# Steps of sorting and of sums queued behind the last instruction of three engines, and ternary weights made among the sorted groups, in a four-layer decoder

## The chip, the cores and the metric

One core of a Trainium2 chip runs the whole decoder as one kernel. The metric is the time of one execution on the device in microseconds (us). The kernel before has a median of 3301.1 us in 15 runs, from 3294.51 to 3314.32. About 0.2% (6.6 us) is what a measurement of this kernel can tell from no change.

## What is computed

A decoder of four layers, each with self-attention, cross-attention and a feed-forward part, and a layer normalization after each of the twelve residual sums. `x` and the context have 128 sequences of 64 tokens of 128 numbers: 8192 tokens, all in float32. The parts that this change touches:

```python
# layer 0, "attention" is a mixture of experts: 8 experts, the best 2 of each token
x = _layernorm(x + _L0_attn_ref(x, gate_w, gate_b, w1, b1, w2, b2))
# layer 0, cross-attention with one head over 64 keys
x = _layernorm(x + _L0_xattn_ref(x, ctx_1024, Wq, bq, Wk, bk, Wv, bv))
# layer 0, feed-forward 128 -> 512 -> 128 with ternary weights
def _ternary(w):
    scale = jnp.maximum(jnp.mean(jnp.abs(w)), 1e-08)
    w_t = jnp.clip(jnp.round(w / scale), -1.0, 1.0)
    return w + jax.lax.stop_gradient(w_t - w)
x = _layernorm(x + _L0_ffn_ref(x, W1, b1, W2, b2))
...
# layer 3: masked cross-attention with 16 heads, then a switch layer (best 1 of 8 experts, with a capacity)
x = _layernorm(x + _L3_xattn_ref(x, ctx_1024, ctx_1024, mask, ...))
x = _layernorm(x + _L3_ffn_ref(x, wg, W1, b1, W2, b2))
```

## The kernel before, in words

**Engines and names.** PE (TensorE) multiplies; `V`, `A` and `G` are VectorE (DVE in the profile), ScalarE (ACT) and GpSimd (POOL); SP issues most DMAs. `x` stays in on-chip memory as 16 chunks `X[0]` to `X[15]` of 512 tokens, each four tiles of 128 tokens.

**Who sets the order.** A scheduler of the tile framework chooses the order of the instructions of each engine from what the Python code traces; it may move an instruction ahead of others traced earlier. Each engine then runs its list strictly in that order. Inside `with tc.issue_after(ins):` every instruction that is traced comes behind `ins` in the list of `ins`'s engine; this is an order, not a wait on a result. `Sorted.after` (used as `moe.after(...)`) is the same for the last instruction that the sorting code kept in `s.pe`, `s.dve`, `s.sp`, `s.gather` or `s.act_ins`.

**The stages** (list `steps` at the end of `tile_decoder`): `moe_top2`, `xattn_single` (cross-attention and ternary feed-forward of layer 0 in one loop), `attn_diff`, `xattn_causal`, `ffn_routed`, `attn_alibi`, `xattn_padded`, `ffn_conv`, `attn_scan`, `xattn_masked`, `ffn_switch`. Ahead of each, `load_weights(n)` (L286) loads a later layer's weights from SP into one of three buffers of the pool `wts`.

**The mixture of experts** (class `Sorted`, `moe`, `moe_top2`) sorts the chosen tokens of a batch of chunks (chunks 0 to 4, then 5 to 15) into groups of 256 rows of one expert: 27 and 51 groups. `all_groups` (L872) walks over the 78 groups: `load` brings the expert's weights (`rw`, 512 KB, SP), `rows` gathers the 256 rows (`aux`, indirect DMAs of POOL, L757, from an index copy `rat` of DVE, L755), `turn` transposes them (`ebT`, L768 and L770), `hidden` and `output` multiply (L782, L795), and `yo` goes to `l_rout` in DRAM (L797). After each group come the `between` hook (here `context`, L917 on: it loads the context) and steps of two generators: the plan of the next batch and the finish of the last one.

**The finish** (`finish`, L803 to L870) is one generator step per tile of 128 tokens plus some at the end. A step copies the row numbers of the tile (`fat`, L815, DVE; four buffers), gathers the two experts' rows (`got`, L817, POOL, two buffers each), adds them to `x` for an earlier tile (L827, L829, DVE), and for each full chunk makes the statistics (L839, L840), the Newton steps of a reciprocal square root (`rsqrt_steps`, L348), and the normalization: `ln_apply` (L371) writes `X[c]` with four instructions, on ACT (`on_act`, L378, with one more DVE product `lns`, L375), or on DVE or POOL (L380). The finish calls it with `on_act=True`. `moe.stretch = 2` leaves about half of batch 0's finish over; `moe_sums` (the generator `moe_end`) holds that remainder and all of batch 1's finish: 11 chunks. `moe_done(c)` (L936) runs it until chunk `c` is normalized.

**The single-head stage** (`xattn_single`, L985 to L1116) runs iterations i from -3 to 17. One iteration traces, for several chunks at once: scores of i+1, the transposed `x` (`turned`) of i-2, the weights, projections of i+2 (bank `v_ps`, L1003), `hidden` of i-2 (first ternary product, L1093, GELU on ACT), `values` of i (L1048; residual `r` L1054; normalization on ACT), `sources` of i+3 (calls `moe_done(i+3)`, transposes the context and `x`, L325 and L332), `output` of i-2 (second ternary product `y`, L1103; residual L399; normalization on DVE for chunks below 8, on POOL from 8 on), with four calls of `summed` between them, one step of `moe_end` each. The ternary weights are made by `ternary(n)` (L1062 to L1080) in iterations -3 and -2; two bias vectors are spread over three bfloat16 rows by `bias_rows` (L966).

**The masked stage** is `mha` (L1130 on) with `aside=kept`: between its parts it runs the first sorting steps of the switch layer (`switch.plan(0)`), each queued behind `seen`, the last instruction of one part of the attention, and `spread`, the last one of a projection.

Of the kernel before, what the change touches and what calls it, by code (L numbers as in the profile page):

```python
# [12 lines left out]
F32 = mybir.dt.float32  # L13
# [4 lines left out]
ALU = mybir.AluOpType  # L18
# [212 lines left out]

@with_exitstack
def tile_decoder(ctx: ExitStack, tc: tile.TileContext, a, out):
    nc = tc.nc
# [6 lines left out]
    dram = ctx.enter_context(tc.tile_pool(name="dram", bufs=1, space=DRAM))  # L243

    mm = nc.tensor.matmul
    V, A, G = nc.vector, nc.scalar, nc.gpsimd


    x_in = a["x"].rearrange("(c t p) d -> c p t d", t=TPC, p=P)
# [35 lines left out]

    def load_weights(n):  # L286

        if 0 < n < 11:
            name = LAYER_WEIGHTS[n - 1]
            parts = []  # L290
            for o in range(0, _NBLOCKS[name], 8):
                k = min(8, _NBLOCKS[name] - o)
                parts.append(work("wts", (P, k, P), f"w_{name}{o}"))
                nc.sync.dma_start(out=parts[-1], in_=a["w_" + name][:, o : o + k, :])
            W[n] = parts[0] if len(parts) == 1 else parts

    def table(name, shape, src):
        t = work("tab", shape, name)
# [6 lines left out]
    def row(n):  # L305
        return rows[:, _ROW_AT[n][0] : _ROW_AT[n][1]]
# [4 lines left out]
    ident = const.tile([P, P], F32, tag="ident", name="ident")  # L311
    make_identity(nc, ident)


    def bank(name):
        return psB.tile([P, 512], F32, tag="m", name=name)
# [155 lines left out]
    class Sorted:  # L472
# [3 lines left out]

        def __init__(s, which, top, batches, src, wg, bias, act, cap=None, store=False, scattered=None):
            s.which, s.top, s.batches, s.src, s.wg, s.bias, s.act, s.cap, s.store = which, top, batches, src, wg, bias, act, cap, store
            s.at, s.loaded, s.done, s.carry = {}, {}, set(), None
# [322 lines left out]
        def finish(s, b):  # L802


            where, share, _, _ = s.at[b]
            K, rows_, cs = s.top, s.count(b) * GR, s.batches[b]
            nt = TPC * len(cs)
            got, sums, ends = {}, {}, []

            def read(n):  # L810
                i, t = divmod(n, TPC)
                if t == 0:
                    got[i] = [work(tag, (P, TPC, D), "got") for tag in ("oT", "ye")[:K]]
                at = sm.tile([P, 2], I32, tag="fat", name="fat", bufs=4)[:, :K]
                s.dve = V.tensor_copy(at, where[:, :, n])  # L815
                for k in range(K):
                    s.gather = G.indirect_dma_start(  # L817
                        out=got[i][k][:, t, :], out_offset=None, in_=s.rout[b][:, :],
                        in_offset=bass.IndirectOffsetOnAxis(ap=at[:, k : k + 1], axis=0), bounds_check=rows_ - 1, oob_is_err=False,
                    )  # L820

            def add(n):
                i, t = divmod(n, TPC)
                if t == 0:
                    sums[i] = work("r", (P, TPC, D)), sm.tile([P, TPC, 6], F32, tag="fst", name="fst")
                r, st = sums[i]
                V.scalar_tensor_tensor(r[:, t, :], got[i][0][:, t, :], share[:, 0, n : n + 1], X[cs[i]][:, t, :], ALU.mult, ALU.add)  # L827
                if K == 2:
                    V.scalar_tensor_tensor(r[:, t, :], got[i][1][:, t, :], share[:, 1, n : n + 1], r[:, t, :], ALU.mult, ALU.add)  # L829
                s.dve = V.bn_stats(st[:, t, :], r[:, t, :])  # L830

            def end(i):
                r, st = sums.pop(i)
                got.pop(i)
                f = sm.tile([P, 4, TPC], F32, tag="fln", name="fln")
                mv = f[:, :2].rearrange("p a t -> p (a t)").rearrange("p (t a) -> p t a", a=2)
                v, y = f[:, 2], f[:, 3]
                for t in range(TPC):
                    V.bn_aggr(mv[:, t, :], st[:, t, :])  # L839
                s.dve = V.tensor_scalar(v, mv[:, :, 1], LN_EPS, None, ALU.add)  # L840
                yield
                for ins in rsqrt_steps(v, TPC, y):
                    s.dve = ins
                    yield
                ln_apply(cs[i], r, mv, y, s.store, on_act=True)
                s.done.add(cs[i])
                yield

            for n in range(nt + LATE + 3):
                if n < nt:  # L850
                    read(n)
# [74 lines left out]
            with moe.after(moe.sp):  # L926
                moe.sp = nc.sync.dma_start(out=CIN[c // 8][:, c % 8 * TPC : (c % 8 + 1) * TPC, :], in_=c_in[c])

    moe.between = context

    def moe_top2():
        for _ in moe.plan(0):
            pass
        moe.all_groups()

    def moe_done(c):  # L936

        while c not in moe.done:
            next(moe_end)


    CTX = [None] * NC
# [38 lines left out]
        return both[:32, 0, :], both[:32, 1, None, :].to_broadcast([32, 4, D])  # L981


    def xattn_single():
        w = W[1]  # L985
        scale = 1.0 / math.sqrt(D)

        st = {}
        bv = bias_rows(row("l0xbv"), 0, "bv1")
        ring = work("e", (P, 4, TPC, D), "v1")  # L990

        def sources(c):
# [62 lines left out]
            layernorm(c, r, on_act=True)  # L1055


        b2 = bias_rows(row("l0fb2"), 1, "b2t")
        tern = W[2]
        wt = work("tab", (P, 2, FK, P), "tern")  # L1060

        def ternary(n):  # L1062
            src = tern[:, 4 * n : 4 * n + 4, :].rearrange("p k m -> p (k m)")
            t = work("tmp", (P, 512), "absw")
            s = sm.tile([P, 1], F32, tag="terns", name="terns")
            A.activation(t, src, AF.Abs)
            V.tensor_reduce(s, t, AX.X, ALU.add)
            ps = bank("tern_ps")
            mm(ps[:, 0:1], sq[:, 2, :], s, start=True, stop=True)

            V.tensor_scalar(s, ps[:, 0:1], 1.0 / (D * FF), 1e-8, ALU.mult, ALU.max)
            V.reciprocal(s, s)
            df = wt[:, n].rearrange("p k m -> p (k m)")
            V.tensor_scalar(df, src, s, None, ALU.mult)
            V.tensor_scalar(df, df, -1.0, 1.0, ALU.max, ALU.min)

            V.tensor_scalar(df, df, 12582912.0, None, ALU.add)
            V.tensor_scalar(df, df, 12582912.0, None, ALU.subtract)
            V.tensor_tensor(df, df, src, ALU.subtract)
            V.tensor_tensor(df, df, src, ALU.add)  # L1080

        def summed(_):
            next(moe_end, None)

        def turned(c):
            st[c] = {"xT": transposed(X[c], "xT")}
# [21 lines left out]
        for i in range(-3, NC + 2):  # L1108
            for step, c in (
# [2 lines left out]
            ):  # L1112
                if step == summed or 0 <= c < NC:
                    step(c)
            if i in (-3, -2):
                ternary(i + 3)  # L1116


    half = const.tile([P, 816], BF16, tag="half", name="half")
# [7 lines left out]
    def rows32(t, g):  # L1127
        return t[32 * g : 32 * g + 32]

    def mha(prepare, wv, finish, mask=None, diff=False, aside=lambda c, k, seen: None):  # L1130

# [165 lines left out]
        on, late, spread = range(NC), (), None  # L1297
        for c in range(-2, NC + 1):
            last = finish(c - 1, st[c - 1]) if c - 1 in on else iter(())
            behind = None  # L1300
            if c in on:
                behind = weights(c, 0)
# [6 lines left out]
            aside(c, 0, (behind, spread))  # L1309
# [5 lines left out]
            aside(c, 1, (seen, spread))  # L1315
            if c in on:
                weights(c, 1)
                behind = values(c, 0)
            aside(c, 2, (behind, spread))
            if c + 1 in on:  # L1320
                scores(c + 1, 1)
                split_maxima(c + 1)
            if c + 2 in on:
                spread = project(c + 2)
            next(last, None)

            seen = maxima(c + 1) if c + 1 in on else None
# [4 lines left out]
            aside(c, 3, (seen, spread))  # L1332
            st.pop(c - 1, None)
        for _ in late:
            pass
# [577 lines left out]
                k = min(16, (n - o) // P)  # L1913
                nc.sync.dma_start(out=x[o : o + k * P, :].rearrange("(k p) d -> p k d", p=P), in_=z[:, None, :].to_broadcast([P, k, D]))

    def kept(c, k, seen):

        last = SWITCH_BATCHES[0][-1]
        n = c - last - 2
        late = [(2, 2, 3, 3), (3, 3, 1, 1), (1, 1, 1, 1), (1, 2, 1, 1), (1, 2, 1, 2), (99, 0, 0, 0)]  # L1920
        steps = 0 if c < 2 else k == 2 if n < 0 else late[n][k]
        with ExitStack() as behind:
            for i in seen:
                if i:
                    behind.enter_context(tc.issue_after(i))
            for _ in range(steps):
                next(switch_begin, None)

    def ffn_switch():
# [34 lines left out]
```

## Time and profile before

| | |
|---|---|
| median of 15 runs | 3301.1 us (3294.51 to 3314.32) |
| the profiled execution | 3298.13 us, span 3296.4, granted clock of TensorE 0.950 |
| PE, DVE, ACT, POOL busy | 2906.6, 2017.0, 1642.5, 1466.0 us |
| groups of the mixture of experts | 53 to 439.5 us, PE busy 336.05 of 386.5 |
| single-head stage | 439.5 to 757 us |
| masked attention, then the switch layer | about 2720 to 3035, then to the end |

How to read it: the page cuts the span into 40 slices of 82.4 us and gives each engine's busy share in tenths; PEclk is the clock that TensorE was granted. Further down it lists groups of instructions: line, engine, operation, what is written `<-` what is read, shapes, count, then busy us and mean ns, and after the bar the engine's idle time just ahead of them and what ended it. A timeline row has start, duration, engine, line, operation, count, and in brackets the idle time ahead. In a table by stretch each row has a stretch, its length, the busy us of PE, PEld (weight loads), DVE, ACT, POOL with counts, then the granted clock, the DMA share and GB/s. A wait line has the engine, the line that waited, the releaser, then us in total, times, longest.

### The profile page before, as it was taken

To read this page: it belongs to the slowest core of one execution; us is meant where nothing else is said; L and a number is where in the kernel's file an instruction comes from. 1 tells how busy PE (TensorE), PEld (TensorE's weight loads), DVE (VectorE), ACT (ScalarE), POOL (GpSimd) and SP (SyncE) were. 2 spreads that over 40 slices of the span, in tenths; PEclk is the share of its full clock that TensorE was granted. 3 is DMA by queue.
4 is the path that set the end of the run, shared out by engine and by line. 5 is a ranking of instruction groups with operands and counts; after the bars stand their busy time and mean duration, and the time that the engine had idled before them with its cause. 6 is when DMAs were issued, how large, how long until landed. Compare 5 with 4: busy or idle time off the path is not lost. (4 is left out here: it accounts for less than half of the span.)

```text
span 3296.4 us, 110598 instructions
## 1 busy us (share of the span) xinstructions
PE 2906.6 (88%) x47136; PEld 2114.6 (64%) x47136; DVE 2017.0 (61%) x7344; ACT 1642.5 (50%) x3138; POOL 1466.0 (44%) x1500
## 2 busy tenths in 40 slices
PE   5888888998899899999999989998999569998983
PEld 3788755565666677766677767774444337766883
DVE  3732256766777566632346665666888886676245
ACT  3443355765544465433345545553445555654443
POOL 2565554334555444311134453557566323436144
PEclk9999988999999899999999999999999789998997
DMA  4567731000000200000000000000000000002684
GB/s 132 158 192 210 226 89 31 20 8 3 3 3 16 78 4 4 6 1 1 1 15 4 4 5 4 4 6 7 1 1 2 8 1 16 18 15 71 191 239 136
DMA packets 142461, 159.26 MB, mean 48 GB/s; under 512 B 16720, under 2 KB 118096, under 8 KB 141968
## 3 DMA queue, kind: packets, MB, share of 16 engines
q1 hardware_dynamic: 128064, 123.66, 13.0%
q0 software_dynamic: 13184, 27.03, 3.2%
q8 instruction: 370, 6.06, 0.8%
q10 hardware_dynamic: 720, 1.50, 0.1%
q14 instruction: 123, 1.01, 0.1%
HBM read 121.45 MB, written 30.67 MB: 46 GB/s over the span
## 5 line engine op out<-in xcount | busy, mean ns | idle before, releaser
L1213 DVE TENSOR_REDUCE m<-s_ps 128x8 f32<-128x512 f32 x640 | 397.4, 683 | 141.7 <-PE s_ps L1441 50.2
L1262 ACT ACTIVATE e<-t_ps 128x512 f32<-128x512 f32 x640 | 330.0, 601 | 149.4 <-PE t_ps L1255 149.0
L1280 PE MATMUL av_ps<-vx,e 128*64 128x18 f32 (+1 forms) x10240 | 338.6, 216 | 8.0 <-issue 7.7
L1280 PEld LDWEIGHTS av_ps<-vx,e 128*64 128x64 f32 x10240 | 320.6, 140 | 28.1 <-issue 20.9
L784 ACT ACTIVATE hT<-h_ps,aux 128x256 f32<-128x256 f32 x496 | 206.8, 470 | 248.2 <-issue 169.2
L1157 POOL TENSOR_SCALAR eb<-qT,small 128x512 f32<-128x512 f32 x80 | 131.3, 1641 | 424.5 <-ACT qT L960 202.6
L817 POOL DMA_INDIRECT got<-l_rout,fat x192 | 192.1, 1001 | 218.6 <-DVE fln L839 63.5
L1243 PE MATMUL t_ps<-eb,kT 32*64 32x128 f32 x10240 | 282.7, 286 | 4.6 <-DVE m L1213 2.3
L380 POOL TENSOR_SCALAR x<-xb,lnmv,ln_y 128x128 f32<-128x128 f32 x240 | 189.3, 801 | 173.9 <-DVE ln_y L345 167.4
L782 PE MATMUL h_ps<-ebT,rw 128*128 128x256 f32 x992 | 245.7, 392 | 17.9 <-DVE ebT L770 14.6
L795 PEld LDWEIGHTS yg<-rw,hT 128*128 128x128 f32 x1984 | 241.7, 192 | 6.7
L1243 PEld LDWEIGHTS t_ps<-eb,kT 32*64 32x64 f32 x10240 | 199.5, 132 | 71.7 <-DVE m L1213 26.1
L795 PE MATMUL yg<-rw,hT 128*128 128x128 f32 x1984 | 241.9, 275 | 0.0
L1205 PE MATMUL s_ps<-eb,qT 32*64 32x256 f32 x5120 | 216.9, 397 | 19.5 <-POOL eb L1157 8.3
L757 POOL DMA_INDIRECT aux<-in_x_dram,rat x156 | 158.8, 1018 | 127.9 <-DVE rat L755 43.4
L782 PEld LDWEIGHTS h_ps<-ebT,rw 128*128 128x128 f32 x992 | 184.6, 196 | 43.7 <-DVE ebT L770 18.8
L380 POOL TENSOR_SCALAR x<-r,lnmv,ln_y 128x128 f32<-128x128 f32 x100 | 79.9, 812 | 293.8 <-DVE ln_y L345 246.7
L1285 DVE RECIPROCAL rc<-av_ps 128x32 f32<-128x32 f32 (+1 forms) x192 | 61.7, 321 | 238.9 <-PE av_ps L1280 238.7
L796 DVE TENSOR_TENSOR yo<-yg,aux 128x256 f32<-128x256 f32 x124 | 52.4, 422 | 251.1 <-PE yg L795 247.8
L1155 ACT ACTIVATE eb<-qT,small 128x512 f32<-128x512 f32 x160 | 106.8, 715 | 128.4 <-POOL qT L1382 123.7
L1157 POOL TENSOR_SCALAR eb<-kT,small 128x512 f32<-128x512 f32 x80 | 145.1, 1814 | 21.1 <-ACT kT L962 11.0
L1205 PEld LDWEIGHTS s_ps<-eb,qT 32*64 32x64 f32 x5120 | 113.8, 133 | 59.4 <-issue 14.8
(443 smaller groups left out, 6495.6 us busy)
## 6 DMA issues: line engine op xcount, KB each, us to landing
rw<-in_l0w_dram SPq DMA_DIRECT2D x78, 512.0 KB
rw<-in_l3w_dram SPq DMA_DIRECT2D x46, 512.0 KB
l_rout<-yo SPq DMA_DIRECT2D x124, 128.0 KB
aux<-xd SPq DMA_DIRECT2D x46, 128.0 KB
aux<-in_l0b_dram SPq DMA_DIRECT2D x78, 66.0 KB
xd<-vx SPq DMA_DIRECT2D x5, 1024.0 KB
x<-in_x_dram SPq DMA_DIRECT2D x16, 256.0 KB
cin<-in_ctx_dram SPq DMA_DIRECT2D x16, 256.0 KB
```

The costliest lines, as they stand in the source:

```text
L380: (V if on_dve else G).tensor_scalar(X[c][:, t, :], r[:, t, :], mv[:, t, 0:1], y[:, t : t + 1], ALU.subtract, ALU.mult)
L757: s.gather = G.indirect_dma_start(out=eb[:, i, :], out_offset=None, in_=x[:, :], in_offset=bass.IndirectOffsetOnAxis(ap=at[:, i : i + 1], ...
L782: s.pe = mm(ps[:, j * GR : (j + 1) * GR], w1[:, (k + j) * P : (k + j + 1) * P], ebT, start=True, stop=True)
L784: s.act_ins = A.activation(hT[k + j], ps[:, j * GR : (j + 1) * GR], s.act, bias=v[:, k + j : k + j + 1])
L795: s.pe = mm(y[:, i * P : (i + 1) * P], hT[k][:, i * P : (i + 1) * P], w2[:, k, :], start=(k == 0), stop=(k == FK - 1))
L817: s.gather = G.indirect_dma_start(out=got[i][k][:, t, :], out_offset=None, in_=s.rout[b][:, :], in_offset=bass.IndirectOffsetOnAxis(ap=at[ ...
L1157: ins = (G if h == 2 else V).tensor_scalar(dst, x, mine, None, ALU.mult)
L1205: mm(ps[g][j * S : (j + 1) * S, u * 256 : (u + 1) * 256].rearrange("p (h k) -> p h k", h=4), rows32(s["q"], g)[:, b], rows32(s["eb"], g)[: ...
L1213: last = V.tensor_reduce(s["m"][:, g, 2 * hf : 2 * hf + 2, :].rearrange("p t h -> p (t h)"), ps[g].rearrange("p (n k) -> p n k", k=S), AX. ...
L1243: mm(ps[g][i * S : (i + 1) * S].rearrange("p (a u j q) -> p a u j q", u=2, a=2, j=2)[:, :, u, j, :], rows32(s["k"], g)[:, b], rows32(s["eb ...
L1262: last = A.activation(e[:, g, :], ps[g], AF.Exp, scale=scale)
L1280: mm(av[j * S : (j + 1) * S, 8 * (u - u0) + n, :], ev[:, n // 2, n % 2, u, j, :], vx[:, 2 * (2 * hf + u) + j, n, :], start=True, stop=True,)
```

## The change

- `V`, `A` and `G` become `Recorded` engines: each keeps the last instruction that was traced on it. `behind(V, A, G)` queues a block behind the last one of each.
- Each `summed` step, each step that `moe_done` runs, and each sorting step of `kept` stands in such a block. The arguments `seen`, `behind` and `spread` of `mha` fall away.
- The ternary weights and the two bias vectors are made in 12 pieces (`made_first`), one at every second of the last 24 groups of the mixture of experts; the weights they need are loaded (`load_weights(2)`) when 30 groups are left, behind the DMAs that the groups put on SP.
- When the groups are done, `moe.slack` is set, and the rest of the finish normalizes on POOL (L380) where it did on ACT (L378).

```diff
+class Recorded:
+    def __getattr__(self, name):
+        method = getattr(self.engine, name)
+        def call(*args, **kwargs):
+            ins = method(*args, **kwargs)
+            self.last = getattr(ins, "ins", None) or self.last
+            return ins
+        return call
...
-    V, A, G = nc.vector, nc.scalar, nc.gpsimd
+    V, A, G = Recorded(nc.vector), Recorded(nc.scalar), Recorded(nc.gpsimd)
...
-        if 0 < n < 11:
+        if 0 < n < 11 and n not in W:
...
+    def behind(*engines):
+        stack = ExitStack()
+        for e in engines:
+            if e.last:
+                stack.enter_context(tc.issue_after(e.last))
+        return stack
...
-                ln_apply(cs[i], r, mv, y, s.store, on_act=True)
+                ln_apply(cs[i], r, mv, y, s.store, on_act=not s.slack)
...
-    moe.between = context
...
         moe.all_groups()
+        assert next(making, None) is None
+        moe.slack = True
...
         while c not in moe.done:
-            next(moe_end)
+            with behind(V, A, G):
+                next(moe_end)
...
+    def ternary(n):
...
+        A.activation(t, src, AF.Abs)
+        yield V.tensor_reduce(s, t, AX.X, ALU.add)
+        ps = bank("tern_ps")
+        moe.pe = mm(ps[:, 0:1], sq[:, 2, :], s, start=True, stop=True)
+        yield
...
+        V.tensor_scalar(df, src, s, None, ALU.mult)
+        yield V.tensor_scalar(df, df, -1.0, 1.0, ALU.max, ALU.min)
+        V.tensor_scalar(df, df, 12582912.0, None, ALU.add)
+        yield V.tensor_scalar(df, df, 12582912.0, None, ALU.subtract)
+        V.tensor_tensor(df, df, src, ALU.subtract)
+        yield V.tensor_tensor(df, df, src, ALU.add)
+
+    def made_first():
+        FIRST["wt"] = work("tab", (P, 2, FK, P), "tern")
+        for n in range(2):
+            yield from ternary(n)
+        FIRST["bv"] = bias_rows(row("l0xbv"), 0, "bv1")
+        yield
+        FIRST["b2"] = bias_rows(row("l0fb2"), 1, "b2t")
+        yield
+
+    making = made_first()
+
+    def before_single(left):
+        context(left)
+        if left == 30:
+            with moe.after(moe.sp):
+                moe.sp = load_weights(2)
+        if left < 24 and left % 2:
+            with behind(V, A, G), moe.after(moe.pe):
+                moe.dve = next(making, None) or moe.dve
+
+    moe.between = before_single
...
+        wt, bv, b2 = FIRST["wt"], FIRST["bv"], FIRST["b2"]
         def summed(_):
-            next(moe_end, None)
+            with behind(V, A, G):
+                next(moe_end, None)
...
-            if i in (-3, -2):
-                ternary(i + 3)
...
-    def kept(c, k, seen):
+    def kept(c, k):
...
-        with ExitStack() as behind:
-            for i in seen:
-                if i:
-                    behind.enter_context(tc.issue_after(i))
-            for _ in range(steps):
+        for _ in range(steps):
+            with behind(V, A, G):
                 next(switch_begin, None)
```

More of the change, by code (lines that the diff above doesn't have):

```diff
@@ L230, in _laid_out, with __init__ @@
     return {n: np.ascontiguousarray(a) for n, a in out.items()}
+class Recorded:
+    def __init__(self, engine):
+        self.engine, self.last = engine, None
+    def __getattr__(self, name):
[5 more added lines that the diff above has]
+        return call
 @with_exitstack
@@ L293, in load_weights @@
                 parts.append(work("wts", (P, k, P), f"w_{name}{o}"))
-                nc.sync.dma_start(out=parts[-1], in_=a["w_" + name][:, o : o + k, :])
+                ins = nc.sync.dma_start(out=parts[-1], in_=a["w_" + name][:, o : o + k, :])
             W[n] = parts[0] if len(parts) == 1 else parts
+            return ins
     def table(name, shape, src):
@@ L478, in __init__ @@
             s.which, s.top, s.batches, s.src, s.wg, s.bias, s.act, s.cap, s.store = which, top, batches, src, wg, bias, act, cap, store
-            s.at, s.loaded, s.done, s.carry = {}, {}, set(), None
+            s.at, s.loaded, s.done, s.carry, s.slack = {}, {}, set(), None, False
             s.row_tiles, s.turned, s.between, s.stretch, s.rest = {}, {}, None, 1, None
@@ L981, in bias_rows @@
         return both[:32, 0, :], both[:32, 1, None, :].to_broadcast([32, 4, D])
+    FIRST = {}
+    def ternary(n):
+        src = W[2][:, 4 * n : 4 * n + 4, :].rearrange("p k m -> p (k m)")
+        t = work("tmp", (P, 512), "absw")
+        s = sm.tile([P, 1], F32, tag="terns", name="terns")
+        A.activation(t, src, AF.Abs)
[3 more added lines that the diff above has]
+        yield
+        V.tensor_scalar(s, ps[:, 0:1], 1.0 / (D * FF), 1e-8, ALU.mult, ALU.max)
+        V.reciprocal(s, s)
+        df = FIRST["wt"][:, n].rearrange("p k m -> p (k m)")
+        V.tensor_scalar(df, src, s, None, ALU.mult)
[22 more added lines that the diff above has]
+    moe.between = before_single
     def xattn_single():
@@ L988, in xattn_single @@
         st = {}
-        bv = bias_rows(row("l0xbv"), 0, "bv1")
         ring = work("e", (P, 4, TPC, D), "v1")
@@ L1055, in values @@
             layernorm(c, r, on_act=True)
[L1058 to L1080, printed above, removed]
+        wt, bv, b2 = FIRST["wt"], FIRST["bv"], FIRST["b2"]
         def summed(_):
-            next(moe_end, None)
+            with behind(V, A, G):
+                next(moe_end, None)
         def turned(c):
@@ L1128, in rows32, with mha @@
         return t[32 * g : 32 * g + 32]
-    def mha(prepare, wv, finish, mask=None, diff=False, aside=lambda c, k, seen: None):
+    def mha(prepare, wv, finish, mask=None, diff=False, aside=lambda c, k: None):
         dh = 16 if diff else 8
@@ L1296, in mha @@
         nlam = lam_neg() if diff else None
-        on, late, spread = range(NC), (), None
+        on, late = range(NC), ()
         for c in range(-2, NC + 1):
             last = finish(c - 1, st[c - 1]) if c - 1 in on else iter(())
-            behind = None
             if c in on:
-                behind = weights(c, 0)
+                weights(c, 0)
             for _ in late:
@@ L1308, in mha @@
                 values(c - 1, 1)
-            aside(c, 0, (behind, spread))
+            aside(c, 0)
             seen = scores(c + 1, 0) if c + 1 in on else None
@@ L1314, in mha @@
                 project_v(c + 1)
-            aside(c, 1, (seen, spread))
+            aside(c, 1)
             if c in on:
                 weights(c, 1)
-                behind = values(c, 0)
-            aside(c, 2, (behind, spread))
+                values(c, 0)
+            aside(c, 2)
             if c + 1 in on:
@@ L1323, in mha @@
             if c + 2 in on:
-                spread = project(c + 2)
+                project(c + 2)
             next(last, None)
@@ L1331, in mha @@
             late = last if diff else ()
-            aside(c, 3, (seen, spread))
+            aside(c, 3)
             st.pop(c - 1, None)
```

## The prediction

> **What bounds the kernel now.** I read the page's forty slices first, then the busy table by stretch, then groups, waits and timelines of the one stage that the change rearranges. The page:
>
> ```profile
> PE   5888888998899899999999989998999569998983
> ...
> POOL 2565554334555444311134453557566323436144
> PEclk9999988999999899999999999999999789998997
> ```
>
> A slice is 82.4 us. TensorE (PE) is nearly full in most slices; POOL is nowhere near it. So TensorE sets the end, and an edit counts only by what it puts on TensorE or keeps it waiting for. The stages touched are the sorting MoE (groups from 53 to 439.5 us), the single-head stage fused with the ternary FFN (439.5 to 757, slices 6 to 9) and the masked attention (about 2720 to 3035). The table by stretch (PE, PEld, DVE, ACT, POOL busy, then granted clock):
>
> ```profile
> 520.00:540.00 20.00, 17.69 (x101) 12.59 (x101) 13.93 (x88) 12.44 (x25) 8.00 (x8) 0.74 0.12 28
> ...
> 560.00:580.00 20.00, 18.12 (x111) 10.88 (x112) 14.29 (x91) 12.19 (x26) 8.00 (x8) 0.83 0.11 27
> ...
> 640.00:680.00 40.00, 40.00 (x310) 27.61 (x312) 30.70 (x186) 32.86 (x65) 6.28 (x8) 1.00 0.01 2
> ```
>
> While the MoE's left-over sums run (to about 620) an iteration of the single-head stage is not bound by TensorE's work: the first products of `hidden` (L1093) start at 503.57 and, seven iterations later, at 636.26: 19.0 us each. Behind them they start at 651.10, 665.98, 680.51: 14.8 us each, at clock 1.00 with PE busy all the time. What holds an iteration at 19 is in the groups of 455 to 640 (busy, mean ns | idle ahead of them, releaser):
>
> ```profile
> L817 POOL DMA_INDIRECT got<-l_rout,fat x88 | 87.9, 999 | 91.9 <-DVE fln L839 62.3 <-issue 20.7 <-DVE fat L815 5.3
> L1103 PE MATMUL y<-tern,vx 128*128 128x128 f32 x256 | 40.3, 318 | 0.0
> ...
> L378 ACT ACTIVATE x<-r,lns,fln 128x128 f32<-128x128 f32 x44 | 19.9, 503 | 0.1
> ...
> L815 DVE COPY fat<-pli 128x2 int32<-128x2 int32 x44 | 7.5, 173 | 39.2 <-DMA got<-l_rout,fat 39.2
> ```
>
> One chunk's finish is eight gathers on POOL (L817); DVE stalls 39.2 us in all for gathers, ahead of the next index copy (L815). POOL's timeline shows the burst, its first and last gather and the next burst:
>
> ```profile
> 545.63 1.01 POOL L817 DMA_INDIRECT got<-l_rout,fat  x1 [9.85 <-DVE fln L839]
> 546.95 1.00 POOL L817 DMA_INDIRECT got<-l_rout,fat  x1 [0.31 <-issue]
> ...
> 554.78 1.00 POOL L817 DMA_INDIRECT got<-l_rout,fat  x1 [0.30 <-issue]
> 565.60 1.01 POOL L817 DMA_INDIRECT got<-l_rout,fat  x1 [9.82 <-DVE fln L839]
> ```
>
> A gather takes 1.30 us from start to start; then POOL idles 9.8. DVE's part: a late index copy, the residual sum of the FFN's output (L399), and that chunk's normalization on DVE:
>
> ```profile
> 558.26 0.17 DVE L815 COPY fat<-pli 128x2 int32<-128x2 int32 x1 [2.20 <-DMA got<-l_rout,fat]
> ...
> 560.06 0.68 DVE L399 TENSOR_TENSOR r<-y,x 128x512 f32<-128x512 f32 x1
> ...
> 566.21 1.09 DVE L380 TENSOR_SCALAR x<-r,lnmv,ln_y 128x128 f32<-128x128 f32 x4
> ```
>
> TensorE pays for the late L399 with a wait for the bank, and a slow stretch behind it:
>
> ```profile
> 560.79 0.37 PE L1003 MATMUL v_ps<-vx 32*128 32x512 bf16 x1 [2.54 <-DVE r L399]
> 561.09 1.20 PE L1008 MATMUL v_ps<-w_l0x,ctx 128*64 128x128 f32 x16
> 562.88 6.61 PE L1093 MATMUL h_ps<-xT,tern 128*128 128x512 f32 x8 [0.58 <-ACT xT L332]
> ```
>
> **The change, part by part.** Counts of the emitted programs: 56 normalizations `x<-r,fln` leave ACT (L378) for POOL, 14 `lns` products vanish from DVE, the multiplications and DMAs stay the same in number.
>
> *1. Order in the single-head stage (decides).* Each `summed` step is now queued behind the last instruction that VectorE, ScalarE and GpSimd got when it was traced, so the order on an engine is fixed where before the scheduler chose. In the changed program an iteration holds, on POOL: x1, two gathers, x2 x3 x4, six gathers. On DVE: L399, statistics, Newton steps, the four normalizations, then index copy #4 (#1 to #4: the copies for the four tiles of a chunk; each feeds two gathers), #1 of the next chunk, the last Newton step of `fln`, #2, #3. On PE: `hidden`, `values`, scores, transpose 1 of a chunk that waits for x1, the first three products of `y`, transposes 2 to 4 (for x2 to x4), and only then the other 13 products of `y` of `output` (each two instructions in the trace). That closes a ring: the end of `y` (call it Y) releases L399; DVE's order puts copy #4 behind the normalizations that follow L399; POOL's order puts x1 to x4 behind gathers that wait for these copies; PE's order puts the next Y behind x4. One turn, from rows:
> - Y to DVE's last normalization: in before 560.06 to 567.30 is 7.24 us, with work of other steps between. Counting only what the new order leaves there I get 6.3 to 6.9; I take 6.5.
> - copy #4: 0.17, say 0.2.
> - four gathers (#4 and the next #1): 4 x 1.30 = 5.2.
> - x1 on POOL. The same operation there, in the stage's later half, is the row below: 0.80.
>
> ```profile
> L380 POOL TENSOR_SCALAR x<-r,lnmv,ln_y 128x128 f32<-128x128 f32 x32 | 25.1, 796 | 68.9 <-PE h_ps L1093 47.0 <-DVE ln_y L345 21.9
> ```
>
> - two gathers 2.6, x2 to x4 2.4.
> - transposes 0.3.
> - 26 instructions of `y`: 3.17 at 552.71 (full clock). Ahead of them PE has now waited about 4 us. After a wait of 3.97 us (at 489.67) 18 of them took 4.21, which makes 26 of them 6.1. Between 3.2 and 6.1 I take 4.3.
>
> Sum 6.5 + 0.2 + 5.2 + 0.8 + 2.6 + 2.4 + 0.3 + 4.3 = **22.3 us** (21.0 to 24.5 by the ends of the terms). In before the ends of `y` go from 498.08 to 646.93 in eight turns, 18.6 each. So 8 x 3.7 = +30 (19 to 47). Two more iterations end the sums: about 19 against 15, and 16 against 15: +5. What goes is DVE's 39.2 us of stalls at L815 and PE's waits for L399 below; late next is POOL's x4.
>
> ```profile
> PE v_ps L1003 <- DVE r L399: 8.9, 5, 2.5
> PE y L1048 <- DVE r L1054: 4.3, 4, 2.0
> ```
>
> *A rule on the clock.* The row: after only 2.54 us of waiting, eight `h_ps` take 6.61 us where in step they take 3.70 (479.43, 543.52, 581.42). The Trainium skill, "TensorE: Matmul & The Clock Gate", Part 1 (What's actually happening), says that the array goes to half clock after an idle window of about 3.4 us; its windows run freely, so it also allows a stretch begun late. By the rule alone, an idle stretch cut in two by transpose 1 could stay at full clock, and a turn would be near 21.2; the rows say otherwise, and I go by them.
>
> *2. The finish's normalizations on POOL.* 56 x 0.80 = 45 us more on POOL, 56 x 0.50 = 28 less on ACT, which was not late (0.1 us idle ahead of these). On POOL they would be free in its 9.8 us of idle time per turn, were it not for their place: 3.2 us of each turn in the sum above are these. Chunk 5 comes ahead of the ring: its 18 gathers end near 497 in before, its normalization needs them partly; I cost nothing beyond the next item.
>
> *3. Ternary weights and bias rows among the MoE's groups.* In before PE waits 4.4 us for `terns` (L1071) near 445, and DVE works some 10 us on them in 440 to 457; both go. The start of the stage is then bound by the gathers of chunk 5 and POOL's x. So the gain up to the second `hidden` is -8 to +4; I take -2. In the groups, twelve pieces come in every second one of the last 24. DVE is busy 148 of 386 us there, so 10 us of ternary and about 5 of bias rows lie beside TensorE; a piece queues its group's `ebT` copies behind it by 0.7 to 1.4 us, and its bank is held for two groups. PE waits there 36.8 us for gathers already, which covers some. I cost it at +2.5 (+1 to +4). The bias rows leave the planning of 121 to 142 us, where PE waited 1.3 and POOL 1.7: -2.5. Together with moe_done's new order: 0 (-4 to +6).
>
> *4. DMAs on SP's queue.* 1002 instructions before and after. The ternary weights go from place 19 to place 317 (behind 50 of 78 expert loads) and the next layer's from 20 to 355; the cross-attention's of layer 1 now stands ahead of the last two expert loads, and must wait until the last ternary piece frees its buffer. If that piece is late, the last expert is late: 0 to +4; I take 0, since the pieces end at the last odd group and three expert buffers are ahead.
>
> *5. Sorting steps in the masked attention.* PE's waits there are 16 us in 315, mostly on `hl` (10.5). Same steps, another place: 0 (-4 to +4).
>
> **Sum**: 30 + 5 - 2 + 0 + 0 + 0 = +33 on the profiled run's 3298.1 us: 3331. That run lies 3 us under the median of 3301.1; on the median's scale 3334.
>
> **Rivals.**
> - *Faster: the ring does not close.* If DVE reaches copy #4 early enough (the new order's stalls are gone, 39.2 us of them) POOL's gathers and x's fit inside an iteration, and TensorE's own 14.8 to 16.5 us set it. Then 8 x (16 - 18.6) = -21, with -2: about 3278. For it: POOL needs only 8 x 1.30 + 4 x 0.80 = 13.6 us a turn. Against it: it needs the chain above 3.7 us shorter merely to break even.
> - *No change: the ring closes at about 18.6*, where before's chain stood: 3301, if the terms of DVE and of `y` are both at less than I read.
> - *Slower still: the clock stays low.* PE works some 14.5 of 22 us at full clock; if the waits hold it at half in most of a turn, `y` takes 6.1 and what precedes x1 (6.61 for `h_ps`) may take over: 24.5 to 26 a turn, +47 to +59, with +3: 3351 to 3363.
> - *SP's queue*: the last expert late by 4 us: adds to any of these.
> - The order of the emitted instructions shows that the change does what it says.
>
> **How the numbers follow.** Forecast (turn of 21 to 24.5): 0.68, 3311 to 3350. Slower still: 0.14. No change, within 0.2% (6.6 us; about what a measurement of this kernel can tell): 0.06. Faster: 0.12. So slower 0.82. The range leaves out the faster case and the top of the slower: 3304 to 3358.
>
> **What would show it.** Right: `x<-r,fln` on POOL between the gathers; PE waiting tens of us for POOL's x at the transposes L325; `hidden` starting every 22 us until some 690, then every 15; no stall at L815 on DVE; a granted clock under 0.9 from 500 to 690; the MoE ending at the same time within 4 us; no wait for `terns`. Wrong: `hidden` at every 16 us or less, or PE waiting for DVE's L399 as before, or a MoE that ends over 6 us later.

## The result, and the profile after

The changed kernel takes 3374.7 us (median of 8 runs, 3365.72 to 3381.46), the kernel before 3302.96 (median of 40). Ratio 1.0216, 95% interval 1.0200 to 1.0232: slower by some 71 us, where the forecast had 33 more and a range that ended at 3358. The direction was right, the size was not.

In the profile after, all instructions of VectorE, ScalarE and GpSimd carry line L243, the one inside `Recorded` that calls the engine; they are told apart by their tiles. Three lines of the page (busy tenths in 40 slices, now of 84.4 us; granted clock last):

```profile
PE   5998877898999899999999989998998669996993
...
POOL 2555555435555444411124453556566223435144
PEclk9999988889999899999999999999998789997997
```

Slices 6 to 9 hold the single-head stage. There TensorE fell from 8, 8, 9, 9 tenths to 7, 7, 8, 9, and its clock from 8, 8, 9, 9 to 8 throughout. The same stretches as before, of the changed kernel:

```profile
520.00:540.00 20.00, 16.01 (x99) 10.73 (x98) 14.44 (x81) 11.09 (x21) 9.53 (x11) 0.84 0.09 23
...
560.00:580.00 20.00, 16.50 (x100) 11.05 (x100) 13.33 (x80) 11.70 (x23) 10.10 (x11) 0.83 0.10 24
...
640.00:680.00 40.00, 32.22 (x196) 20.58 (x194) 29.29 (x172) 21.61 (x41) 19.66 (x21) 0.83 0.09 24
```

The counts say more than the busy times: 196 matmuls in the last stretch where there were 310, since before the sums had ended by then (last gather at 632.0 us) and now have not (697.2). The groups of 455 to 640:

```profile
L243 POOL DMA_INDIRECT got<-l_rout,fat x74 | 75.6, 1021 | 75.6 <-DVE r L243 56.2 <-issue 14.8 <-DVE fln L243 1.4
L1149 PE MATMUL y<-tern,vx 128*128 128x128 f32 x218 | 45.4, 392 | 0.0
...
L243 POOL TENSOR_SCALAR x<-r,fln 128x128 f32<-128x128 f32 x36 | 29.0, 812 | 3.7 <-DVE fln L243 3.1
...
L243 DVE COPY fat<-pli 128x2 int32<-128x2 int32 x35 | 5.8, 170 | 0.0
```

DVE's stall at the index copies is gone (39.2 to 0.0). In its place TensorE waits for POOL's normalizations, ahead of the transposes:

```profile
PE xT_ps L349 <- POOL x L243: 45.8, 45, 3.5
PE xT_ps L349 <- ACT x L243: 4.5, 1, 4.5
```

`y` takes 392 ns an instruction where it took 318. One turn of the ring, first on POOL (start, duration, and the idle time ahead in brackets):

```profile
579.32 0.99 POOL L243 DMA_INDIRECT got<-l_rout,fat  x1 [8.57 <-DVE r L243]
...
583.22 0.99 POOL L243 DMA_INDIRECT got<-l_rout,fat  x1 [0.30 <-issue]
584.25 0.81 POOL L243 TENSOR_SCALAR x<-r,fln 128x128 f32<-128x128 f32 x1
585.23 1.08 POOL L243 DMA_INDIRECT got<-l_rout,fat  x1 [0.17 <-DVE lnst L243]
...
587.66 2.35 POOL L243 TENSOR_SCALAR x<-r,fln 128x128 f32<-128x128 f32 x3
```

then on TensorE, which waits for x1 and again for x2 to x4, and runs the rest of `y` at a low clock (26 instructions in 5.16 us, 3.17 in step):

```profile
585.11 0.47 PE L349 MATMUL xT_ps<-ident,x 128*128 128x128 f32 x1 [3.40 <-POOL x L243]
...
588.52 0.48 PE L349 MATMUL xT_ps<-ident,x 128*128 128x128 f32 x1 [0.82 <-POOL x L243]
...
590.33 5.16 PE L1149 MATMUL y<-tern,vx 128*128 128x128 f32 x26
```

The clock granted from 584.5 to 594.7 was 0.50 (third figure from the end):

```profile
584.50:594.70 10.20, 8.17 (x32) 6.63 (x33) 2.86 (x17) 0.58 (x1) 7.08 (x8) 0.50 0.12 32
```

and on DVE, with copy #4 behind the normalizations, and L399 (here `r<-y,x`) waiting for `y`:

```profile
577.86 1.12 DVE L243 TENSOR_SCALAR x<-r,lnmv,ln_y 128x128 f32<-128x128 f32 x4
578.89 0.16 DVE L243 COPY fat<-pli 128x2 int32<-128x2 int32 x1
...
595.53 0.69 DVE L243 TENSOR_TENSOR r<-y,x 128x512 f32<-128x512 f32 x1 [7.89 <-PE y L1149]
```

Where the 79.5 us between the two spans (3296.4 and 3375.9) came in, by the starts or ends of the same products in both traces:

| landmark | before | after | later by |
|---|---|---|---|
| end of the groups (first transposed `x`) | 439.92 | 440.89 | 1.0 |
| end of `y` for chunk 0 | 498.09 | 503.61 | 5.5 |
| end of `y` for chunk 8, eight turns on | 646.93 | 687.11 | 40.2 |
| end of `y` for chunk 10 | 676.11 | 729.86 | 53.8 |
| end of the stage (last `y`) | 727.26 | 779.87 | 52.6 |
| start of the masked stage | 2708.22 | 2765.54 | 57.3 |
| its last product | 3034.41 | 3100.42 | 66.0 |
| last product of the gates of the switch layer | 3066.59 | 3145.63 | 79.0 |

So 52 us belong to the single-head stage and 22 to the masked stage and the sorting behind it. Five came between, in stages that the change does not touch: these take 1981.0 us before and 1985.7 after, and between 1975 and 1990 in the runs below. Nine of the 22 lie inside the masked stage and 13 behind it, where TensorE waits for the first sorted rows (`xd`), before and after:

```profile
PE ebT_ps L768 <- DMA aux<-xd: 3.3, 1, 3.3
```

```profile
PE ebT_ps L792 <- DMA aux<-xd: 15.5, 1, 15.5
```

### The profile page after: what moved, and what is told of

The parts are those of the page before. It is cut to its first block, busy times and chain, and to the rows that moved or that the text cites. A ratio compares the mean times of both kernels' runs of the same rounds, so it can differ in the third digit from the quotient of the medians.

```text
span 3375.9 us, 110652 instructions
## 1 busy us (share of the span) xinstructions
PE 2946.2 (87%) x47136; PEld 2140.8 (63%) x47136; DVE 2035.7 (60%) x7330; ACT 1620.7 (48%) x3082; POOL 1510.6 (45%) x1556
## 5 line engine op out<-in xcount | busy, mean ns | idle before, releaser
L243 DVE TENSOR_REDUCE m<-s_ps 128x8 f32<-128x512 f32 (+1 forms) x656 | 403.9, 676 | 149.9 <-PE s_ps L1584 49.9
L243 ACT ACTIVATE e<-t_ps 128x512 f32<-128x512 f32 x640 | 329.8, 601 | 154.2 <-PE t_ps L1299 153.8
L243 ACT ACTIVATE hT<-h_ps,aux 128x256 f32<-128x256 f32 x496 | 206.5, 469 | 253.8 <-issue 175.7
L243 POOL TENSOR_SCALAR eb<-qT,small 128x512 f32<-128x512 f32 x80 | 131.4, 1642 | 427.8 <-ACT qT L243 349.7
L243 POOL DMA_INDIRECT got<-l_rout,fat x192 | 194.6, 1013 | 228.4 <-DVE r L243 128.9
L243 POOL TENSOR_SCALAR x<-xb,lnmv,ln_y 128x128 f32<-128x128 f32 x240 | 188.0, 795 | 177.8 <-DVE ln_y L243 174.2
L806 PE MATMUL h_ps<-ebT,rw 128*128 128x256 f32 x992 | 247.2, 394 | 16.3 <-DVE ebT L243 12.9
L243 POOL DMA_INDIRECT aux<-in_x_dram,rat x156 | 159.1, 1020 | 129.7 <-DVE rat L243 45.4
L243 POOL TENSOR_SCALAR x<-r,lnmv,ln_y 128x128 f32<-128x128 f32 x100 | 79.8, 810 | 288.5 <-DVE ln_y L243 261.6
L243 DVE TENSOR_TENSOR yo<-yg,aux 128x256 f32<-128x256 f32 x124 | 52.4, 423 | 258.3 <-PE yg L819 258.1
L243 DVE RECIPROCAL rc<-av_ps 128x32 f32<-128x32 f32 (+1 forms) x192 | 61.7, 321 | 242.1 <-PE av_ps L1324 241.7
L243 ACT COPY xT<-xT_ps 128x512 f32<-128x512 f32 x128 | 77.0, 602 | 241.3 <-PE xT_ps L349 241.3
L243 ACT ACTIVATE eb<-qT,small 128x512 f32<-128x512 f32 x160 | 106.8, 715 | 128.6 <-POOL qT L243 123.7
L243 POOL TENSOR_SCALAR eb<-kT,small 128x512 f32<-128x512 f32 x80 | 145.1, 1814 | 21.5 <-ACT kT L243 19.2
```

The source lines that it names most:

```text
L243: ins = method(*args, **kwargs)
L806: s.pe = mm(ps[:, j * GR : (j + 1) * GR], w1[:, (k + j) * P : (k + j + 1) * P], ebT, start=True, stop=True)
```

## The experiments

Two things are needed to read them. A ratio stands against the kernel before **on the same chip**. And the kernel before took 3295 to 3303 us on most of the chips, 3375 and 3378 on two others; a time from these two says nothing beside the table above. The first four runs fell on one of the two.

**kept_as_before, norm_on_act, sums_free, ternary_moved_alone.** The edits, to the changed kernel (the last one has all three of them, so only the ternary weights and bias rows are moved):

In kept_as_before `kept` and the loop of `mha` are again those of the kernel before:

```diff
-    def kept(c, k):
+    def kept(c, k, seen):
...
-        for _ in range(steps):
-            with behind(V, A, G):
+        with ExitStack() as behind:
+            for i in seen:
+                if i:
+                    behind.enter_context(tc.issue_after(i))
+            for _ in range(steps):
                 next(switch_begin, None)
```

In norm_on_act the left-over normalizations stay on ACT:

```diff
-        moe.slack = True
```

In sums_free `summed`, and `moe_done` likewise, lose their order:

```diff
-            with behind(V, A, G):
-                next(moe_end, None)
+            next(moe_end, None)
```

> The changed kernel with only the sorting steps of the masked stage put back behind the attention's own instructions (kept as before). Theory A (the 22 us that the time line shows later in the masked stage and behind it, 8 up to its end and 13 between its last product and the first sorted group, come from the new place of these steps: the ten index casts on DVE are spread, so the forty scatters on POOL start and end later): 3374.7 - 22 = 3353 us (3349 to 3358). Rival B (they are a consequence of the later start or of noise): 3370 to 3380.

> The changed kernel with only the left-over normalizations back on ACT; the queueing behind the last instructions stays. Theory A (the ring of 22.9 us closes through POOL's normalizations, which stand between gathers): without them POOL has only gathers, an iteration falls under 18.6 us, the single-head stage ends 45 to 65 us earlier than in the changed kernel: 3312 to 3332 us. Rival B (the queueing itself closes the ring, by DVE's index copies behind its normalizations): an iteration stays at 20 or more: 3355 to 3375 us.

> The changed kernel without the queueing of summed and moe_done; normalizations stay on POOL. The scheduler then puts the four normalizations of a chunk behind its eight gathers, and TensorE's transposes of them behind each other. Theory A (the place between the gathers and the early transposes make the ring): an iteration at 18.6 to 20, 3330 to 3345 us. Rival B (any normalization on POOL costs its 3.2 us in each turn and more): 21 to 23 us an iteration, 3355 to 3375 us.

> The kernel before with only the ternary weights and bias rows made among the sorted groups (with their load moved); normalizations on ACT, sums and sorting steps as before. Theory A (what the trace shows: 4.4 us of waiting for the ternary scale goes, the groups end 1 us later, so 3 to 4 us are gained and later hidden in part by the gathers): 3294 to 3302 us. Rival B (the gathers bind the stage's start, nothing is gained): 3302 to 3306.

Measured: 3405.29, 3372.96, 3371.34 and 3376.97 us beside 3375.18 of the kernel before; ratios 1.0096 (1.0069 to 1.0124), 0.9992 (0.9973 to 1.0012), 0.9986 (0.9970 to 1.0003), 0.9995 (0.9979 to 1.0011). The expected times were worked out for the other chips and can't be held against these. What these four can still tell: taking the normalizations off POOL, or freeing the sums, is worth some 1% against kept_as_before, which keeps both. The rest was measured again on other chips.

**before_again, after_again, norm_act_kept_as_before, sums_free_kept_as_before**, side by side on another chip. The third has `slack` off and `kept` as before; the fourth has the sums free and `kept` as before.

> The kernel before itself, for its profile on this chip. In the four runs above the kernel before took 3375 us beside them, 72 us more than in the runs of the result, and their traces show idle time of DVE and TensorE that is put down to issue (39 to 78 us on DVE, 41 to 61 on TensorE), where the two first profiles have none on DVE. Theory A (a matter of the chip): the kernel before shows such idle time too where its time is near 3375, and none where it is near 3300. Rival B (a matter of the edited kernels): none on DVE whatever its time.

> The changed kernel itself on the same chip as the next two. Theory A (its ring in the single-head stage and the late scatters cost about the same on any chip): 65 to 80 us above the kernel before on this chip (ratio 1.020 to 1.024). Rival B (on a chip where instructions are late the two are hidden in part by that): ratio 1.00 to 1.015.

> The changed kernel with the left-over normalizations back on ACT and the sorting steps of the masked stage as before; what is left of the change is the queueing of the sums and the moved ternary weights. Theory A (normalizations on POOL make the ring, the late scatters the rest): ratio to the kernel before 0.990 to 1.000. Rival B (the queueing of the sums alone closes a ring): 1.006 to 1.015.

> The changed kernel without the queueing of the sums and with the sorting steps as before; what is left is the normalizations on POOL, placed by the scheduler behind all eight gathers of a chunk, and the moved ternary weights. Theory A (the ring needs both the place between gathers and POOL): ratio to the kernel before 0.993 to 1.004. Rival B (any normalization on POOL costs its 3.2 us in each of eight turns): 1.006 to 1.012.

Measured: before_again 3300.31, with no idle time of DVE put down to issue; both theories allow that at 3300 us, so it decides nothing between them. after_again 3374.94, ratio 1.0226 (1.0190 to 1.0263), theory A; the two traces repeat the first pair (eight turns of 18.6 and 22.8 us, the masked stage in 325.5 and 335.0). norm_act_kept_as_before 3278.59, ratio **0.9939** (0.9915 to 0.9963), theory A: **faster than both kernels**. Its waits of TensorE from 455 to 700, and POOL's next bursts:

```profile
PE xT_ps L349 <- ACT x L243: 7.5, 10, 1.4
PE y L1114 <- DVE fln L243: 2.8, 4, 0.8
PE v_ps L1069 <- DVE r L243: 2.5, 2, 1.4
```

```profile
544.75 1.00 POOL L243 DMA_INDIRECT got<-l_rout,fat  x1 [4.46 <-DVE r L243]
...
553.96 1.00 POOL L243 DMA_INDIRECT got<-l_rout,fat  x1 [0.30 <-issue]
561.07 1.00 POOL L243 DMA_INDIRECT got<-l_rout,fat  x1 [6.11 <-DVE r L243]
```

The bursts are 16.3 us apart (20.0 before), `hidden` starts every 15.5 us from 527.22 to 620.37 with a granted clock of 1.00, and TensorE waits 7.5 us in all for normalizations where the changed kernel waits 45.8. The queueing, with the moved weights, is a gain of 20 us; queue_alone below has it without them.

sums_free_kept_as_before: 3319.18, ratio 1.0056 (1.0037 to 1.0075): neither theory. Its turns take 19.3 us (522.28 to 637.90, six of them), near the 18.6 of the kernel before, but the first `hidden` starts at 502.81, 23 us after the kernel before's 479.43. Most of that is not POOL's: up to there TensorE waits 3.8 us for its normalizations, and 16.0 for two others, `kT` and `x` of ScalarE, that ternary_alone_2 below shows too (17.2), with the normalizations on ACT.

```profile
PE xT_ps L349 <- POOL x L243: 3.8, 4, 2.6
PE s_ps L1087 <- ACT kT L243: 11.0, 2, 7.7
PE xT_ps L349 <- ACT x L243: 5.0, 1, 5.0
```

The two kernels differ in these normalizations alone, and 1.0056 against 1.0031 is some 8 us, with intervals that overlap. So normalizations on POOL cost little where nothing puts them between the gathers.

**norm_on_act_2, norm_act_casts_free, norm_twice, ternary_alone_2**, side by side on a third chip.

norm_act_casts_free is norm_on_act with another order in `kept`; norm_twice changes `ln_apply` for the left-over normalizations alone:

```diff
-            with behind(V, A, G):
+            with behind(A, G):
                 next(switch_begin, None)
```

```diff
-                (V if on_dve else G).tensor_scalar(X[c][:, t, :], ...)
+                for _ in range(2 if twice else 1):
+                    (V if on_dve else G).tensor_scalar(X[c][:, t, :], ...)
```

> The changed kernel with only the left-over normalizations back on ACT (the queueing, the moved ternary weights and the new place of the sorting steps stay), on another chip than the first time. Beside it stands what was measured with the sorting steps as before as well: 0.9939 of the kernel before. Theory A (the late scatters cost 13 to 22 us whatever happens in the single-head stage): ratio 0.998 to 1.001. Rival B (they cost that only after a late start): ratio 0.992 to 0.996.

> As norm_on_act_2, but the sorting steps of the masked stage are queued only behind ScalarE's and GpSimd's last instructions, not behind VectorE's: all fourteen casts of the row numbers then stand together on DVE, ahead of where the kernel before has most of them. Theory A (the scatters are late because the casts are spread behind the attention's DVE work): the scatters run at 1.28 us each without gaps, ratio 0.990 to 0.995. Rival B (the scatters are late because of their own place on POOL): as norm_on_act_2.

> The changed kernel with each left-over normalization on POOL written twice, which changes no value: four more instructions of 0.8 us in each chunk, 44 in the ring. Theory A (a closed ring through POOL, slope one): 3.2 us more in each of ten iterations, 3375 + 32 = 3407 us (3400 to 3415). Rival B (POOL's idle time of some 8 us in an iteration hides them): 3375 to 3382.

> The kernel before with only the ternary weights and bias rows made among the sorted groups, on another chip than the first time. Theory A (4.4 us of waiting goes, 1 to 2 us come back in the groups): ratio 0.998 to 1.000. Rival B (the gathers bind the start of the stage): 1.000 to 1.003.

*norm_on_act_2*: 3296.14, ratio 0.9989 (0.9976 to 1.0002), theory A: the new place of the sorting steps costs 0.5% (16 us) with a fast single-head stage too.

*norm_act_casts_free*: 3298.31, ratio 1.0000 (0.9987 to 1.0013): no gain over norm_on_act_2, so theory A's ratio fell. The scatters did run without gaps and early, from 2943.23 on; but they then stood ahead of what the attention needs from POOL (`eb`, the scaled queries and keys), and TensorE waited there:

```profile
2943.23 1.11 POOL L243 DMA_INDIRECT xd<-x,pli  x1 [0.31 <-DVE pli L243]
...
2963.73 1.59 POOL L243 TENSOR_SCALAR eb<-qT,small 128x512 f32<-128x512 f32 x1
```

```profile
PE s_ps L1248 <- POOL eb L243: 20.1, 2, 14.9
```

From the start of the masked stage to its last product it lost 19 us on the kernel before, and nothing behind it. So the delay was moved, not taken away: forty scatters, 1.28 us from start to start, are 51 us of POOL, and the attention needs POOL in that time too.

*norm_twice*: 3419.53, ratio 1.0360 (1.0337 to 1.0382), 45 us above the changed kernel's 3374.9: theory A's ring, with a slope above one, so 4.5 us above the top of its range. `hidden` starts every 26.8 us (516.10 to 703.87) instead of 22.8, four us for 3.2 of added work: TensorE waits longer, and the clock granted over these turns is 0.75 where the changed kernel has 0.80 (531 to 714):

```profile
608.32 5.61 POOL L243 TENSOR_SCALAR x<-r,fln 128x128 f32<-128x128 f32 x7
```

```profile
PE xT_ps L349 <- POOL x L243: 104.1, 51, 8.4
```

*ternary_alone_2*: 3307.24, ratio 1.0031 (1.0017 to 1.0045): neither a gain nor nothing, but 10 us lost. The wait for `terns` is gone, and two others stand in its place, for ScalarE, while the first chunks are normalized:

```profile
PE s_ps L1086 <- ACT kT L243: 10.0, 3, 5.9
PE xT_ps L349 <- ACT x L243: 7.2, 1, 7.2
```

The first `hidden` starts 15.5 us late. At the end of the stage 3.6 of it are left beside the first profile of the kernel before, 10.1 beside that of before_again: two profiles of one kernel differ there by 6.5 us.

**queue_alone, kept_alone, norm_dve_kept_as_before**, side by side. The first two are the kernel before with one part of the change; the third is the changed kernel with

```diff
-                ln_apply(cs[i], r, mv, y, s.store, on_act=not s.slack)
+                ln_apply(cs[i], r, mv, y, s.store, on_act=not s.slack, on_dve=s.slack)
```

and with `kept` as before.

queue_alone, against the kernel before (with `Recorded` and `behind` added), and the same in `moe_done`; kept_alone has the new `kept` and `mha` of the change in the same way:

```diff
-            next(moe_end, None)
+            with behind(V, A, G):
+                next(moe_end, None)
```

> The kernel before with only the left-over sums queued behind the last instructions of the three engines; ternary weights, normalizations on ACT and sorting steps as before. With the ternary weights moved as well the ratio was 0.9939, and these moved alone gave 1.0031. Theory A (the two add): ratio 0.989 to 0.9925. Rival B (the queueing already took what the moved weights cost, or needs them out of the way): 0.993 to 0.997.

> The kernel before with only the sorting steps of the masked stage in their new place. Theory A (their cost does not depend on what comes before: 16 us between norm_on_act_2 and norm_act_kept_as_before, 22 us on the time line of the changed kernel): ratio 1.004 to 1.007. Rival B (it depends on it): 0.999 to 1.002.

> The changed kernel with the left-over normalizations on DVE in place of POOL and the sorting steps as before. On DVE four take about 1.1 us where POOL needs 3.2, and they stand behind no gather. Theory A (POOL's place between the gathers makes the ring of 22.9 us): the ring is gone, ratio 0.992 to 0.999. Rival B (taking them off ACT, or DVE's own load, costs): 1.003 or more.

*queue_alone*: 3278.02, ratio 0.9919 (0.9899 to 0.9940): theory A by its middle, though the interval reaches into B. *kept_alone*: 3321.75, ratio 1.0061 (1.0044 to 1.0079), theory A: 20 us, of which its landmarks put 6 inside the masked stage and 13 behind it. The first group of the switch layer waits for the scattered rows, as in the changed kernel:

```profile
PE ebT_ps L792 <- DMA aux<-xd: 15.5, 1, 15.5
```

*norm_dve_kept_as_before*: 3273.03, ratio **0.9906** (0.9880 to 0.9931), the lowest ratio of all: theory A. Waits of TensorE for normalizations there:

```profile
PE xT_ps L349 <- DVE x L243: 10.4, 9, 2.3
```

**queue_norm_dve, queue_norm_dve_2**: queue_alone with the left-over normalizations on DVE, that is, the kernel above with the ternary weights as before.

> The kernel before with the left-over sums queued and their normalizations on DVE once the groups are done; ternary weights and sorting steps as before. Theory A (the moved weights cost some 6 us under the queueing, as 0.9919 against 0.9939 may say): ratio 0.986 to 0.990. Rival B (they cost nothing there): 0.990 to 0.993.

> As queue_norm_dve, on another chip: there the kernel before took 3378 us beside it, 77 us more than in the other jobs, as it did in the first four runs. Theory A (the moved weights cost some 6 us under the queueing): ratio 0.986 to 0.990 where the kernel before takes near 3300. Rival B (nothing): 0.990 to 0.993.

The first fell on a chip where the kernel before took 3377.89: 3371.51, ratio 0.9982 (0.9968 to 0.9995). The second: 3269.46, ratio 0.9931 (0.9909 to 0.9954), at the upper edge of rival B; all of theory A's range lies below the interval. On ACT the moved weights seem to cost (0.9939 against 0.9919), on DVE to gain (0.9906 against 0.9931); both pairs overlap. What they cost or gain under the queueing stays open.

## Why the forecast was right in direction and wrong in size

**The ring (part 1): right but for its last term.** The turn from 572.68 to 595.49, with the forecast in brackets: `y` to the last normalization on DVE 6.2 (6.5), copy #4 0.4 (0.2), four gathers 4.9 (5.2), x1 1.0 (0.8), two gathers 2.4 (2.6), x2 to x4 2.4 (2.4), transposes 0.3 (0.3), `y` 5.2 (4.3): 22.8 (22.3). The mean of eight turns is 22.9, and 8 x 4.3 = 34.7 where the forecast had 30. What was mis-sized is the last term, `y` behind a wait: I took 4.3 between 3.2 and 6.1, and it takes 5.16. The upper bound was stretched from the first 18 products after the wait at 489.67; the row itself goes on, at full clock from some 497.1 on, and its first 26 products take 5.4 us:

```profile
492.11 5.98 PE L1103 MATMUL y<-tern,vx 128*128 128x128 f32 x30
```

By the rule alone (the Trainium skill, "TensorE: Matmul & The Clock Gate", Part 1, What's actually happening: half clock after an idle window of about 3.4 us) the forecast's estimate of a turn was 21.2 us. The turn measured 22.8, but it does not tell the rule from the rows, since its first wait is already 3.40 us. The kernel before does: behind the wait of 2.54 us its granted clock was 0.50 from 562.0 to 568.7, so the rows were the better guide. norm_twice shows the ring closed; norm_act_kept_as_before and norm_dve_kept_as_before open it by moving the normalizations, with the queueing left in, and sums_free_kept_as_before by taking the queueing away, with the normalizations left on POOL.

**Its end: mis-sized.** "About 19 against 15, and 16 against 15: +5" measured 22.5 and 20.3 against 15.4 and 13.8: +13.6. The chunks that are left keep nearly the full ring until the last gather; I let it fade.

**The start of the stage (part 3): wrong sign.** "I take -2" was +4.1 at the second `hidden` (503.57 and 507.66) and +5.5 at the end of `y` for chunk 0. The 4.4 us wait went, as said. What came in its place are mostly waits for POOL's normalizations: 8.1 us of TensorE up to 505, and norm_on_act_2, which has them on ACT and everything else of the change, starts its first `hidden` at 476.69, ahead of the changed kernel's 484.04 (481.19 in after_again). That I had written off as "I cost nothing beyond the next item". The moved weights cost 10 us by themselves (ternary_alone_2), but norm_on_act_2 shows no such delay under the queueing.

**The masked stage (part 5): the step that failed.** "Same steps, another place: 0 (-4 to +4)" is 22 us on the time line and 20 by kept_alone. It is the largest single miss, and without it the total would have lain inside the range. I looked at TensorE's waits (16 us in 315) and not at POOL, which has forty scatters to issue in the stage's last 60 us, and I did not count what stands behind the waiting casts. In the kernel before, the scatters run from

```profile
2972.11 1.12 POOL L655 DMA_INDIRECT xd<-x,pli  x1 [5.57 <-DVE pli L654]
...
3034.93 0.97 POOL L655 DMA_INDIRECT xd<-x,pli  x1 [0.31 <-issue]
```

and end with the stage. In the changed kernel they start 62 us later, five more than the stage does, and end 78 us later:

```profile
3034.24 1.11 POOL L243 DMA_INDIRECT xd<-x,pli  x1 [12.76 <-DVE pli L243]
...
3113.30 0.97 POOL L243 DMA_INDIRECT xd<-x,pli  x1 [0.30 <-issue]
```

Each cast on DVE now stands behind the attention's instruction traced just ahead of it, and the scatters come in bursts of 2 to 10, with 2.1 to 6.0 us of idle POOL ahead of several of them. The first group of the switch layer waits for the last of them (15.5 us where it waited 3.3). That the spread casts are the reason is argued from the order and the trace; norm_act_casts_free, which put the casts together, only moved the wait to another place.

**SP's queue (part 4): right.** The groups end 1.0 us later, and no expert load is waited for.

**The rivals.** "Faster: the ring does not close" was the right picture of the queueing itself, at 15.5 to 16.4 us a turn and 20 to 31 us gained. Two things kept it from being the result: the normalizations on POOL (after_again against norm_on_act_2 is 1.0226 against 0.9989, some 78 us) and the sorting steps (16 to 20 us). "Slower still: the clock stays low" gave 24.5 to 26 a turn; the turns were 22.9. Its time, 3351 to 3363, is nearer to the result than the forecast's, but by terms that it does not have. In us of 3300, from ratios on different chips: queueing -27, sorting steps +20, so -7 together, where the two with the moved weights measured -4 (norm_on_act_2); with the normalizations on POOL, +78, the change measured +71 to +75.

## What to carry to other kernels

A fixed order can close a loop: write down one turn engine by engine, and see what stands behind what. Where the loop is closed, the sum of its terms is the time of an iteration (here 22.3 forecast, 22.9 measured), whatever the busy shares say. Idle time of an engine (POOL's 9.8 us a turn in the kernel before) is no room for more work if the work must stand in the middle of that engine's list, in the chain. For a step that is moved, count what it issues on every engine (here forty scatters), not what the busiest engine waits for.

## What the runs showed that was not expected

On two chips the kernel before takes 3375.18 and 3377.89 us, 2.3% more than on the others, and the profiles taken there show TensorE idle for 41 to 61 us with nothing in the profile that it waited for (8 to 13 us elsewhere), mostly in the single-head stage and at the end of the masked one. An instance, from ternary_moved_alone:

```profile
445.83 1.11 PE L1073 MATMUL v_ps<-w_l0x,ctx 128*64 128x128 f32 x6 [5.44 <-issue]
450.17 2.07 PE L980 MATMUL qT_ps<-xT,w_l0x 128*128 128x512 f32 x2 [3.23 <-issue]
```

What holds the engine there is not known; POOL has gathers or scatters running in both stretches. The kernel before was not profiled on these chips. And moving the normalizations from ACT to DVE cost nothing that shows (0.9906 against 0.9939), though DVE was the busier of the two in that stretch before (13.9 of 20 us against 12.4).
